# A state-space mixer on one core: the rows of B in their own PSUM bank, the block boundary in pieces

## The chip, the core and the metric

The kernel runs on one core of a Trainium2 chip. The core has five engines with instruction queues of their own: PE (matmul, with its weight loads shown apart as PEld), DVE (vector), ACT (activation functions), POOL (general vector work) and SP (here it only starts DMAs). Each engine works through its queue in order; semaphores make it wait for others. Matmul results land in PSUM, which has eight banks of 128 x 512 fp32; DVE and ACT read PSUM, POOL does not in this program. The metric is the time of one execution on the device in microseconds (us); of several runs the median is given.

## The reference, cut to what matters

The program is a stack of four layers, each a mixer and a feed-forward part, all with a residual and a norm before and after. The change touches the last mixer (a selective state-space model, "mamba") and the start of the feed-forward part behind it (routing to 8 experts). There are 8 batches of 512 tokens, width 256, inner width 512, 16 states. For each batch:

```python
xr = x @ W_in.T                       # x is the layernorm of the residual
xc, res = xr[..., :512], xr[..., 512:]
u = silu(depthwise_conv4(xc) + b_conv)
dt, B, C = split(u @ W_xproj.T)       # 16 + 16 + 16
delta = softplus(dt @ W_dt.T + b_dt)
dA = exp(delta * A)                   # per channel and state
dBu = delta * B * u
h_t = dA_t * h_(t-1) + dBu_t          # scan over 512 tokens
y = sum_n h * C + u * D
out = (y * silu(res)) @ W_out.T
x = x + layernorm(out)
```

The next part begins with `scores = softmax(layernorm(x) @ w_router)` and the two best experts of each token.

## The kernel before

Everything here is fp32. A block is one batch, b = 0 to 7; channels lie on the partitions in four chunks c of 128, tokens along the free dimension. `l3_attn` (L1545) walks a list of 128 pairs (b, n), a block's 16 states one after another (L1690).

**One state.** For each chunk ACT makes dA = exp(A dl) into PSUM (L1703, two tiles) and DVE scans it with dB into half of an h tile (L1706). POOL multiplies the two h tiles, 128 x 1024 each, by the row of C (L1709), and PE adds them into four PSUM banks y with an identity as weights (`summed`, L1677); this sum stands one state later in the program. h has six tiles, that is three states. What a scan takes is prepared two states ahead by `inputs` (L1642): the row of C comes by DMA from a DRAM copy of the projection, spread over the partitions (L1646, four tiles). For an even state PE spreads the row of B into PSUM with a one-column selection (pb, L1649) and DVE multiplies it by du (dB, L1652); for an odd state a DMA brings the row (L1656) and POOL multiplies (L1657).

**The next block's front.** `front` (L1590) is a generator that is stepped once per state while block b is scanned, and makes what block b+1 needs. It normalises x (`norm_act`: statistics on DVE, the scaling xn on ACT, L160), transposes it (L146, copied to xT, L148), and for each chunk projects (pi, L1585), copies to xc (L1596), convolves by four diagonal matmuls (pc, L1599) and copies to u with the bias (L1602). Then come Silu on u (L1604) with a load of ACT's table before and after it, the projection px (L1609), its copy xd and the DMA of xd to DRAM (L1616). For each chunk of delta one matmul pd (L1622), five ACT operations (L1627 to L1631) and three of DVE (L1633 to L1635) make the softplus dl. At last POOL forms du = dl u in one instruction of 128 x 2048 (L1638).

**The boundary.** In state 0 of block b the old block is finished: DVE gates y with sr (L1667), PE starts the new y with u D (L1715), `out` projects the old block back (py, L190) and `add_norm` (L164) takes statistics on DVE (L105 to L115, L170), scales on ACT (yn, L177) and adds to the residual X on POOL (L179). yn has the same buffer as xn. Then the gate of block b is projected (L1721, pi again) and goes through its own Silu (L1722), with two table loads.

**Banks.** PSUM is full: two banks "mm", two for dA, four for y. In "mm" stand pxT, pi, pc, px, pd, py and pb, in turn.

**Order.** The source order is a priority, not the queue: a scheduler at build time puts an instruction ahead where by its own reckoning its operands and buffers are there. So in the trace statistics of X for later blocks, and for the routing of the next part (`route`, L1812; `norm`, L126), stand amid the scans as soon as X is ready. Table loads keep their place in the program (L123).

Of the kernel before, what the change touches and what calls it, by code (L numbers as in the profile page):

```python
# [9 lines left out]
F32 = mybir.dt.float32  # L10
# [35 lines left out]
class Kern:  # L46


    def __init__(self, ctx, tc, i):
        self.ctx, self.tc, self.nc, self.i = ctx, tc, tc.nc, i  # L50
        nc = self.nc
        self.const = ctx.enter_context(tc.tile_pool(name="const", bufs=1))
        self.xpool = ctx.enter_context(tc.tile_pool(name="xres", bufs=1))
        self.wpool = ctx.enter_context(tc.tile_pool(name="wts", bufs=1))
        self.small = ctx.enter_context(tc.tile_pool(name="small", bufs=3))
        self.dram = ctx.enter_context(tc.tile_pool(name="dram", bufs=1, space=DRAM))
        self.C = self.const.tile([P, 384], F32, name="C")
        nc.sync.dma_start(out=self.C, in_=i["consts"][:, 0:384])
        self.ident = self.C[:, C_ID:C_ID + 128]
        self.caus = self.C[:, C_CAUS:C_CAUS + 128]  # L60
        self.up = self.C[:, C_UP:C_UP + 128]
        self.ones = self.const.tile([1, 128], F32, name="ones")
        nc.vector.memset(self.ones, 1.0)
        self.XA = self.xpool.tile([P, NB, NT, D], F32, name="X")
        self.X = [self.XA[:, b] for b in range(NB)]
        self.W = {}

        self.log_exp = False
        self.eps = self.const.tile([P, 1], F32, name="eps")
        nc.vector.memset(self.eps, LN_EPS)  # L70

# [51 lines left out]
        self.tc.keep_in_program_order(  # L123
            self.nc.scalar.preload_act_table_set("natural_log_exp_and_others"))

    def norm(self, b, pool):  # L126

        nc = self.nc
        x = self.X[b]
        mv, r = self.stats([x[:, n, :] for n in range(NT)], "ln")  # L130
        xn = pool.tile([P, NT, D], F32, tag="xn", name=f"xn{b}")
        for n in range(NT):
            nc.vector.tensor_scalar(
                xn[:, n, :], x[:, n, :], mv[:, n, 0:1], r[:, n:n + 1], ALU.subtract, ALU.mult)
        return xn
# [12 lines left out]
            nc.scalar.copy(xT[:, k, :], ps)  # L148
        return xT

    def norm_act(self, b, pool):

        nc = self.nc
        x = self.X[b]
        mv, r = self.stats([x[:, n, :] for n in range(NT)], "ln")
        nb = self.small.tile([P, NT], F32, tag="lnb", name="lnb")
        nc.vector.scalar_tensor_tensor(nb, mv[:, :, 0], -1.0, r, ALU.mult, ALU.mult)
        xn = pool.tile([P, NT, D], F32, tag="xn", name=f"xn{b}")
        for n in range(NT):
            nc.scalar.activation(  # L160
                xn[:, n, :], x[:, n, :], AF.Identity, bias=nb[:, n:n + 1], scale=r[:, n:n + 1])
        return xn
# [1382 lines left out]
def l3_attn(K):  # L1545

    nc, tc = K.nc, K.tc
    w = K.W["l3_attn"]  # L1550
    win = w[:, 0:2048].rearrange("p (k n) -> p k n", k=2)
# [3 lines left out]
    with ExitStack() as es:  # L1555
# [1 line left out]
            return es.enter_context(tc.tile_pool(name="l3" + name, bufs=bufs, **kw))  # L1557
        cst, s1, s2, s3 = pool("c", 1), pool("a", 1), pool("b", 2), pool("d", 3)
        s4, s6 = pool("h", 4), pool("g", 6)
        pmm = pool("pm", 2, space=PSUM)  # L1560
        pA = pool("pa", 2, space=PSUM)
        pY = pool("py", 1, space=PSUM)
        dr = pool("dr", 2, space=DRAM)
# [23 lines left out]
                    start=(k == 0), stop=(k == 1))  # L1587
            return ps

        def front(b, res):  # L1590
            xT = K.norm_T(
                b, s1, pmm, "mm", xn=K.norm_act(b, s1), dst=s1.tile([P, 2, L], F32, tag="xT", name=f"xT{b}"))
            yield
            u = s1.tile([P, 4, L], F32, tag="u", name=f"u{b}")
            for c in range(4):
                nc.scalar.copy(xc[:, 3:], project_in(b, c, xT))  # L1596
                pc = pmm.tile([P, L], F32, tag="mm", name=f"pc{b}_{c}")
                for s in range(4):
                    nc.tensor.matmul(  # L1599
                        pc, lhsT=dg[:, c, s, :], rhs=xc[:, 3 - s:3 - s + L],  # L1600
                        start=(s == 0), stop=(s == 3))
                nc.scalar.activation(u[:, c, :], pc, AF.Identity, bias=W[:, c, M_BC:M_BC + 1])  # L1602
                yield
            nc.scalar.activation(flat(u), flat(u), AF.Silu)  # L1604
            K.log_exp_tables()
            yield
            px = pmm.tile([48, L], F32, tag="mm", name=f"px{b}")
            for c in range(4):
                nc.tensor.matmul(  # L1609
# [7 lines left out]
            yield  # L1617

            dl = s2.tile([P, 4, L], F32, tag="dl", name=f"dl{b}")
            for c in range(4):  # L1620
                ps = pmm.tile([P, L], F32, tag="mm", name=f"pd{b}_{c}")
                nc.tensor.matmul(  # L1622
                    ps, lhsT=wdt[:, c * P:(c + 1) * P], rhs=xd[0:16, :], start=True, stop=True)
                bd = W[:, c, M_BD:M_BD + 1]
                e = s2.tile([P, L], F32, tag="e", name=f"e{b}_{c}")
                lg = s2.tile([P, L], F32, tag="lg", name=f"lg{b}_{c}")
                nc.scalar.activation(e, ps, AF.Abs, bias=bd)  # L1627
                nc.scalar.activation(dl[:, c, :], ps, AF.Relu, bias=bd)
                nc.scalar.activation(e, e, AF.Exp, scale=-1.0)
                nc.scalar.activation(ps, e, AF.Identity, bias=1.0)  # L1630
                nc.scalar.activation(lg, ps, AF.Ln)  # L1631

                nc.vector.scalar_tensor_tensor(ps, ps, -1.0, e, ALU.add, ALU.subtract)  # L1633
                nc.vector.tensor_tensor(ps, lg, ps, ALU.subtract)
                nc.vector.tensor_tensor(dl[:, c, :], ps, dl[:, c, :], ALU.add)  # L1635
                yield
            du = s2.tile([P, 4, L], F32, tag="du", name=f"du{b}")
            nc.gpsimd.tensor_tensor(flat(du), flat(dl), flat(u), ALU.mult)  # L1638
            res.update(xT=xT, u=u, dl=dl, du=du, xd=xd,
                       rows=xd_d.rearrange("(j n) t -> n j t", j=2))  # L1640

        def inputs(b, n):  # L1642
            du, xd, rows = res[b]["du"], res[b]["xd"], res[b]["rows"]
            dB = s3.tile([P, 4, L], F32, tag="dB", name=f"dB{b}_{n}")
            C = s4.tile([P, L], F32, tag="C", name=f"C{b}_{n}")
            nc.sync.dma_start(out=C, in_=rows[n, 1].partition_broadcast(P))  # L1646
            if n % 2 == 0:
                pb = pmm.tile([P, L], F32, tag="mm", name=f"pb{b}_{n}")
                nc.tensor.matmul(  # L1649
                    pb, lhsT=K.ident[0:48, 16 + n:17 + n].to_broadcast([48, P]), rhs=xd,  # L1650
                    start=True, stop=True)
                nc.vector.tensor_tensor(  # L1652
                    dB, du, pb[:, None, :].to_broadcast([P, 4, L]), ALU.mult)
            else:
                B = s2.tile([P, L], F32, tag="B", name=f"B{b}_{n}")
                nc.sync.dma_start(out=B, in_=rows[n, 0].partition_broadcast(P))  # L1656
                nc.gpsimd.tensor_tensor(  # L1657
                    dB, du, B[:, None, :].to_broadcast([P, 4, L]), ALU.mult)
            return dB, C

        def out(b, yT):
            K.project_out(
                b, [(yT[:, c, :], W[:, c, M_OUT:M_OUT + D]) for c in range(4)], pmm, "mm", s1, tag="xn")

        def gate(b, py, sr):
            for c in range(4):
# [3 lines left out]
        def summed(state):  # L1670
# [4 lines left out]
            for j, h in enumerate(hs):  # L1675
                for c in range(2):
                    nc.tensor.matmul(  # L1677
                        py[2 * j + c], lhsT=K.ident, rhs=h[:, c, :], start=False,
                        stop=(n == NS - 1))

        res = [{} for _ in range(NB)]
        for _ in front(0, res[0]):
            pass
        order = [(b, n) for b in range(NB) for n in range(NS)]
        ready = {k: inputs(*k) for k in order[:2]}
        py = sr = last = None
        nxt = iter(())
        for k, (b, n) in enumerate(order):  # L1690
            if n == 0:
                nxt = front(b + 1, res[b + 1]) if b + 1 < NB else iter(())
                dl, u = res[b]["dl"], res[b]["u"]
            if n == NS - 2:
                for _ in nxt:
                    pass
            dB, C = ready.pop((b, n))
            if k + 2 < len(order):
                ready[order[k + 2]] = inputs(*order[k + 2])
            hs = []  # L1700
            for c in range(4):
                dA = pA.tile([P, L], F32, tag="dA", name=f"dA{b}_{n}_{c}")
                nc.scalar.activation(dA, dl[:, c, :], AF.Exp, scale=A[:, c, n:n + 1])  # L1703
                if c % 2 == 0:
                    hs.append(s6.tile([P, 2, L], F32, tag="h", name=f"h{b}_{n}_{c}"))
                nc.vector.tensor_tensor_scan(  # L1706
                    hs[-1][:, c % 2, :], dA, dB[:, c, :], 0.0, ALU.mult, ALU.add)
            for h in hs:
                nc.gpsimd.tensor_tensor(h, h, C[:, None, :].to_broadcast([P, 2, L]), ALU.mult)  # L1709
            summed(last)  # L1710
            if n == 0:
                yT = gate(b - 1, py, sr) if b else None
                py = [pY.tile([P, L], F32, tag=f"y{c}", name=f"y{b}_{c}") for c in range(4)]
                for c in range(4):
                    nc.tensor.matmul(  # L1715
                        py[c], lhsT=dg[:, c, 4, :], rhs=u[:, c, :], start=True, stop=False)
                if b:
                    out(b - 1, yT)
                sr = s1.tile([P, 4, L], F32, tag="sr", name=f"sr{b}")
                for c in range(4):  # L1720
                    nc.scalar.copy(sr[:, c, :], project_in(b, 4 + c, res[b]["xT"]))  # L1721
                nc.scalar.activation(flat(sr), flat(sr), AF.Silu)  # L1722
                K.log_exp_tables()
            last = (py, hs, n)
            next(nxt, None)
        summed(last)
        out(NB - 1, gate(NB - 1, py, sr))
        K.log_exp = False


# [1 line left out]
def l3_ffn(K):  # L1732
# [18 lines left out]
    with ExitStack() as es:  # L1751
# [59 lines left out]

        def route(b, sb):  # L1812

            xn = K.norm(b, sb)
            nc.sync.dma_start(
                out=xn_d[b * L:(b + 1) * L].rearrange("(n p) d -> p n d", p=P), in_=xn)
            t = K.norm_T(b, sb, pmm, "mm", xn=xn, dst=TS[b])
# [340 lines left out]
```

## Time and profile before

| | us |
|---|---|
| median of 3 runs | 5200.95 |
| lowest and highest run | 5196.74, 5203.29 |
| the profiled execution | 5193.12 |
| its span, first to last instruction | 5191.4 |
| mean granted PE clock over the span | 0.927 of full |
| PE, DVE, ACT, POOL busy over the span | 4407.5, 3047.7, 1928.3, 1865.3 |
| scans (L1706), first to last start | 3431.7 to 4523.0 |
| C-products on POOL (L1709), last start | 4531.1 |

The times in a profile are of the one profiled execution; they are compared with its own span, not with the median. A group's line gives the code line, engine, operation, the tile written and those read, the shape and the count, then the busy time and the mean of one in ns, then the idle time of the engine just before them and what ended most of it. A wait is put down to what ended it, so an engine that waits in its queue also holds everything behind it. Busy spans of one engine can overlap by up to 0.1 us where instructions are pipelined. In the mixer the four y banks, the h tiles and the "mm" banks tie the engines together: each is handed on only when its last reader is done.

### The profile page before, as it was taken

How to read it: one execution, taken by the hardware profiler on the slowest of the kernel's cores; microseconds unless marked ns; L12 is line 12 of the kernel's file. 1: busy time of each engine (PE TensorE's matmuls, PEld its weight loads, DVE VectorE, ACT ScalarE, POOL GpSimd, SP SyncE). 2: the span in 40 equal slices, each digit the busy share in tenths (PEclk: the TensorE clock that was granted, in tenths of full speed). 3: DMA queues.
4: the chain of work that ended last, by engine and by line, in shares of the span. 5: the costliest groups of instructions: out<-in, count | busy, mean ns of one | idle time of the engine just before them, and what ended most of it. 6: DMA issues, size and time to landing. Idle time of an engine off the chain costs nothing.

```text
span 5191.4 us, 56559 instructions
## 1 busy us (share of the span) xinstructions
PE 4407.5 (85%) x18804; PEld 2700.6 (52%) x18804; DVE 3047.7 (59%) x8229; ACT 1928.3 (37%) x3817; POOL 1865.3 (36%) x1201
## 2 busy tenths in 40 slices
PE   8745789999983996988888899988888888899998
PEld 3334675565552894544444455533333333368885
DVE  7999646466687113555555653357778877761115
ACT  5401323434341332433333333355555555321112
POOL 0001213444342343111111110057889887803331
PEclk9876899999996997999999999999999999899999
DMA  4397411000001893000000000011111111126763
GB/s 113 80 208 176 132 47 48 5 5 9 5 17 42 225 253 97 5 5 5 5 5 5 1 20 1 0 43 42 45 45 49 45 43 43 47 80 216 227 214 101
DMA packets 401528, 357.89 MB, mean 69 GB/s; under 512 B 209394, under 2 KB 334020, under 8 KB 400676
## 3 DMA queue, kind: packets, MB, share of 16 engines
q1 hardware_dynamic: 373236, 305.83, 21.2%
q0 software_dynamic: 16320, 31.65, 2.2%
q10 hardware_dynamic: 11680, 16.80, 1.0%
q8 instruction: 149, 2.44, 0.2%
q14 instruction: 143, 1.17, 0.1%
HBM read 287.87 MB, written 66.09 MB: 68 GB/s over the span
## 4 chain that ended last, share of the span: by engine, by line
PE 34%; DVE 18%; issue 6%; POOL 5%; ACT 3%; DMA 1%; DVEq 0%; POOLq 0%; ACTq 0%; SPq 0%
DVE h L1706 7%; PE gb L1785 4%; PE T L1421 4%; PE h L1240 3%; DVE junk L1391 3%; PE g L1534 3%; PE y L1677 3%; PE yb L1799 2%; DVE dB L1652 2%; PE py L190 2%; PE pc L1599 2%; PE y L1251 2%; POOL h L1709 2%; PE o L1411 1%; PE pi L1585 1%
## 5 line engine op out<-in xcount | busy, mean ns | idle before, releaser
L1709 POOL TENSOR_TENSOR h<-h,C 128x1024 f32<-128x1024 f32 x256 | 596.2, 2357 | 178.2 <-DVE h L1706 140.0
L1677 PE MATMUL y<-h,C 128*128 128x512 f32 x1024 | 530.9, 659 | 104.6 <-POOL h L1709 104.6
L1706 DVE TENSOR_TENSOR_SCAN h<-dA,dB 128x512 f32<-128x512 f32 x512 | 589.4, 1204 | 29.4 <-ACT dA L1703 11.7
L1703 ACT ACTIVATE dA<-dl,A 128x512 f32<-128x512 f32 x512 | 352.5, 691 | 411.4 <-DVE h L1706 410.8
L935 POOL TENSOR_SCALAR p<-p,rs 128x128 f32<-128x128 f32 (+3 forms) x256 | 276.3, 1088 | 385.6 <-DVE rs L934 226.0
L1677 PEld LDWEIGHTS y<-h,C 128*128 128x128 f32 x1024 | 201.0, 207 | 410.9 <-issue 222.0
L1424 ACT ACTIVATE PT<-T 128x256 f32<-128x256 f32 (+3 forms) x512 | 208.5, 438 | 416.4 <-PE T L1421 409.8
L179 POOL TENSOR_TENSOR X<-X,yn 128x1024 f32<-128x1024 f32 x64 | 151.2, 2363 | 559.8 <-ACT yn L177 483.2
L1386 PE MATMUL S<-KT,qz 128*128 128x512 f32 (+3 forms) x1024 | 321.2, 453 | 22.4 <-DVE mx L1391 8.7
L1421 PE MATMUL T<-qz,KT 128*128 128x512 f32 (+3 forms) x1024 | 320.4, 445 | 12.0 <-ACT PT L1424 9.3
L1426 POOL TENSOR_SCALAR_AFFINE_SELECT PT<-PT 128x512 f32<-128x512 f32 x128 | 81.1, 637 | 609.8 <-ACT PT L1424 609.8
L1657 POOL TENSOR_TENSOR dB<-du,B 128x2048 f32<-128x2048 f32 x64 | 289.8, 4529 | 0.1
L1391 DVE CUSTOM_DVE_ANT_0 junk<-S,mask 128x256 f32<-128x256 f32 (+3 forms) x512 | 251.4, 491 | 61.9 <-PE S L1386 4.9
L1785 PE MATMUL gb<-xbT,w_b 128*128 128x256 f32 (+1 forms) x1472 | 255.3, 332 | 1.0 <-ACT ts L1989 0.6
L1386 PEld LDWEIGHTS S<-KT,qz 128*128 128x128 f32 x1024 | 180.4, 191 | 142.4 <-DVE mx L1391 30.7
L1652 DVE TENSOR_TENSOR dB<-du,pb 128x2048 f32<-128x2048 f32 x64 | 145.5, 2275 | 170.2 <-PE pb L1649 120.3
L1785 PEld LDWEIGHTS gb<-xbT,w_b 128*128 128x128 f32 x1472 | 230.2, 191 | 23.1 <-ACT ts L1989 0.8
L1791 DVE TENSOR_TENSOR hTb<-sb,gb 128x512 f32<-128x512 f32 x71 | 48.9, 688 | 325.3 <-PE gb L1785 325.3
L1421 PEld LDWEIGHTS T<-qz,KT 128*128 128x128 f32 x1024 | 169.1, 191 | 132.4 <-issue 66.5
L933 ACT ACTIVATE p<-p,nm 128x128 f32<-128x128 f32 (+3 forms) x256 | 143.8, 563 | 198.8 <-DVE nm L929 193.5
L1245 ACT ACTIVATE hT<-h,w_l_ffn 128x128 f32<-128x128 f32 x384 | 109.8, 368 | 220.3 <-PE h L1240 220.3
L1240 PE MATMUL h<-xgT,w 128*128 128x128 f32 x1536 | 185.0, 279 | 0.0
(506 smaller groups left out, 9132.7 us busy)
## 6 DMA issues: line engine op xcount, KB each, us to landing
w_b<-l3f_w SPq DMA_DIRECT2D x138, 512.0 KB
w<-l1f_w SPq DMA_DIRECT2D x48, 1024.0 KB
C<-xdd SPq DMA_DIRECT2D x128, 256.0 KB
B<-xdd SPq DMA_DIRECT2D x64, 256.0 KB
w<-l1f_w SPq DMA_DIRECT2D x48, 256.0 KB
toep<-l0fd SPq DMA_DIRECT2D x32, 320.0 KB
X<-x SPq DMA_DIRECT2D x16, 512.0 KB
toep<-l0fd SPq DMA_DIRECT2D x32, 256.0 KB
```

The source lines that it names most:

```text
L935: nc.gpsimd.tensor_scalar(p[:, 0:n], p[:, 0:n], rs, None, ALU.mult)
L1240: nc.tensor.matmul(ph[:, j, :], lhsT=w1[:, s, c, m * P:(m + 1) * P], rhs=xgT[:, c, :], start=(c == 0), stop=(c == 1))
L1386: nc.tensor.matmul(ps[:, 0:n], lhsT=QZ[:, j, qt * P:n], rhs=KT[:, g, 0:n], start=True, stop=True)
L1391: nc.vector.tensor_tensor_reduce(out=junk[:, 0:n], in0=tiles[j][:, 0:n], in1=mask[:, L - n:L], scale=1.0, scalar=-3.0e38, op0=ALU.add, op1 ...
L1421: nc.tensor.matmul(ps[:, 0:n], lhsT=KT[:, g, kt * P:(kt + 1) * P], rhs=QZ[:, j, kt * P:L], start=True, stop=True)
L1652: nc.vector.tensor_tensor(dB, du, pb[:, None, :].to_broadcast([P, 4, L]), ALU.mult)
L1657: nc.gpsimd.tensor_tensor(dB, du, B[:, None, :].to_broadcast([P, 4, L]), ALU.mult)
L1677: nc.tensor.matmul(py[2 * j + c], lhsT=K.ident, rhs=h[:, c, :], start=False, stop=(n == NS - 1))
L1703: nc.scalar.activation(dA, dl[:, c, :], AF.Exp, scale=A[:, c, n:n + 1])
L1706: nc.vector.tensor_tensor_scan(hs[-1][:, c % 2, :], dA, dB[:, c, :], 0.0, ALU.mult, ALU.add)
L1709: nc.gpsimd.tensor_tensor(h, h, C[:, None, :].to_broadcast([P, 2, L]), ALU.mult)
L1785: nc.tensor.matmul(ps[:, q, :], lhsT=ww[:, k, (c + q) * P:(c + q + 1) * P], rhs=xT[:, k, :], start=(k == 0), stop=(k == 1))
```

## The change

- PSUM: "mm" has one bank, and a pool "pb" of one bank holds the rows of B of even states.
- `inputs` is split. `rows_of` (DMA of C, and B by PE or DMA) runs three states ahead, `product` (dB) two ahead; both now stand after a state's four scans, where `inputs` stood before them.
- `front` is stepped after the second scan of each state but the first, not at a state's end. xn is written into the upper half of the tile that u will fill. A chunk's conv and the next chunk's projection form one piece. The gate's Silu of block b and the Silu of u of block b+1 stand together. lg lies in du's chunk, e has one tile, and du is formed chunk by chunk (four of 128 x 512). The gate's projection for b+1 is the last piece.
- `among` wraps this: norm of b+1, then the projection back of b-1 (now with leave=True, so ACT first copies the two PSUM halves to SBUF, L175), then the rest of `front`.
- In the last block, where there is no front, `among` makes the statistics of X[0] to X[6] for the next part, one batch per state, each behind a fence: a DVE memset that keeps its place in the program. They are copied to constant tiles, and `route` takes them from there.

The core of the diff:

```diff
+    def fence(self):
+        t = self.small.tile([P, 1], F32, tag="fence", name="fence")
+        return self.tc.keep_in_program_order(self.nc.vector.memset(t, 0.0)).ins
+
-        mv, r = self.stats([x[:, n, :] for n in range(NT)], "ln")
+        mv, r = known or self.stats([x[:, n, :] for n in range(NT)], "ln")
...
-        pmm = pool("pm", 2, space=PSUM)
+        pmm = pool("pm", 1, space=PSUM)
+        pB = pool("pb", 1, space=PSUM)
...
+            u = s1.tile([P, 4, L], F32, tag="u", name=f"u{b}")
+            xn = K.norm_act(b, s1, u[:, 2:4, :].rearrange("p c t -> p (c t)").rearrange(
+                "p (n d) -> p n d", n=NT))
+            yield
...
-            nc.scalar.activation(flat(u), flat(u), AF.Silu)
+            for t in (sr, u):
+                if t is not None:
+                    nc.scalar.activation(flat(t), flat(t), AF.Silu)
             K.log_exp_tables()
...
-            nc.gpsimd.tensor_tensor(flat(du), flat(dl), flat(u), ALU.mult)
+                nc.gpsimd.tensor_tensor(du[:, c, :], dl[:, c, :], u[:, c, :], ALU.mult)
+            yield
+            for c in range(4):
+                nc.scalar.copy(res["sr"][:, c, :], project_in(b, 4 + c, xT))
+                if c == 1:
+                    yield
...
+        def among(b, yT):
+            sr = res[b]["sr"]
+            ahead = front(b + 1, res[b + 1], sr) if b + 1 < NB else iter(())
+            next(ahead, None)
+            if b:
+                out(b - 1, yT)
+            yield
+            if b + 1 < NB:
+                yield from ahead
+            else:
+                nc.scalar.activation(flat(sr), flat(sr), AF.Silu)
+                K.log_exp_tables()
+                for d in range(NB - 1):
+                    yield
+                    mv = K.const.tile([P, NT, 2], F32, name=f"fmv{d}")
+                    r = K.const.tile([P, NT], F32, name=f"fr{d}")
+                    K.known.append((mv, r))
+                    with tc.issue_after(K.fence()):
+                        m, t = K.stats([K.X[d][:, n, :] for n in range(NT)], "ln")
+                        nc.vector.tensor_copy(mv, m)
+                        nc.vector.tensor_copy(r, t)
...
+                if n and c == 1:
+                    next(nxt, None)
...
+            if k + 2 < len(order):
+                ahead = order[k + 2]
+                dBs[ahead] = product(*ahead, rows[ahead][0])
+            if k + 3 < len(order):
+                rows[order[k + 3]] = rows_of(*order[k + 3])
```

## The prediction

> **What bounds it now.** I read the share table first, and it misleads: over the span PE is busiest, but the change lies in the state-space mixer alone, from about 3368 to 4545 us of the profiled execution (the stretch where the scan's line appears). So I took that stretch by blocks. The scans' starts in order of time give block starts at 3431.7, 3550.0, 3693.2, 3836.4, 3979.6, 4123.5, 4266.8 and 4410.3: block 0 takes 118.2 us, the six blocks after it 143.2 to 143.9 (mean 143.4). The view by stretches has block 0, block 2 and block 7 to the end of POOL's work (length, then busy us and count of PE, PEld, DVE, ACT, POOL, then the granted clock):
>
> ```profile
> 3431.70:3550.00 118.30, 104.76 (x223) 39.57 (x221) 95.49 (x85) 70.41 (x104) 107.56 (x40) 0.95 0.19 51
> 3693.20:3836.40 143.20, 124.19 (x273) 50.53 (x272) 107.86 (x116) 75.93 (x115) 116.82 (x43) 0.92 0.18 45
> 4410.30:4533.40 123.10, 97.36 (x204) 41.20 (x202) 97.16 (x90) 52.56 (x76) 114.99 (x43) 0.86 0.14 42
> ```
>
> POOL carries the most: 116.8 of 143.2 us. It is 32 products with C, 8 odd dB, du and one residual add, in the page's rows:
>
> ```profile
> L1709 POOL TENSOR_TENSOR h<-h,C 128x1024 f32<-128x1024 f32 x256 | 596.2, 2357 | 178.2 <-DVE h L1706 140.0
> ...
> L1657 POOL TENSOR_TENSOR dB<-du,B 128x2048 f32<-128x2048 f32 x64 | 289.8, 4529 | 0.1
> ...
> L1652 DVE TENSOR_TENSOR dB<-du,pb 128x2048 f32<-128x2048 f32 x64 | 145.5, 2275 | 170.2 <-PE pb L1649 120.3
> ```
>
> The last row shows the cause: DVE lost 120 us to pb. Who waited in block 2, POOL's three waits and DVE's largest two (total, times, longest):
>
> ```profile
> POOL h L1709 <- DVE h L1706: 22.5, 4, 18.1
> POOL h L1709 <- DVE onb L170: 2.8, 1, 2.8
> POOL h L1709 <- PE pb L1649: 1.1, 1, 1.1
> ```
>
> ```profile
> DVE dB L1652 <- PE pb L1649: 15.9, 2, 12.0
> DVE dB L1652 <- POOL du L1638: 6.4, 1, 6.4
> ```
>
> So POOL idles 26.4 us per middle block, 18.1 at once. The chain of waits through that hole (start, us, what):
>
> ```profile
> 3726.31 2.31 POOL X L179
> 3728.62 0.03 issue
> 3728.65 0.60 ACT xn L160
> ...
> 3729.77 3.71 PE pi L1585 x8
> ...
> 3741.74 3.52 PE pc L1599 x8
> 3745.26 1.06 PE pb L1649 x2
> 3746.32 0.02 issue
> 3746.34 2.30 DVE dB L1652
> ```
>
> A row of B (pb) takes its bank from the ring "mm" that pxT, pi, pc and py use. Here it queues behind the next block's front; the front waits for xn, whose buffer is still yn until the add to X; and DVE holds scans behind the dB that wants pb. Block 0 has the same front but no block before it to finish, and no such hole: its first eight states take 58.5 us, block 2's 84.3; its last eight 59.7, block 2's 58.9.
>
> **The change, part by part.** *B rows in an own bank, three ahead; norm in u; no hoisted routing statistics.* These cut every link of that chain: pb needs only the even dB of two states before; xn no longer waits for the add; and the next layer's statistics (bn_stats on X, where DVE idles 4.9 us for the add in block 2) are fenced into block 7. POOL's floor becomes 32 x 2.31 (starts of products back to back) + 8 x 4.49 + 2.30 + du. du in pieces: 2.357 at 1024 and 4.529 at 2048 give 0.18 + 2.12 per 1024, so 1.24 for 512, 5.0 for four instead of 4.5. Floor 117.1. For what idles above it I take block 0's halves: 58.5 + 2.3 (add) + 2.8 (DVE's onb wait stays) + 59.0 + 0.5 = 123.1. With 1 us for the ring below: **124 per middle block, 19.4 less, six times: -116**. Ends: floor and 2 us (119), and 143.
>
> *Ring of one bank instead of two.* Per block it is handed on 21 times (2 pxT, 8 pi, 4 pc, px, 4 pd, 2 py). A handover is an ACT copy and two hops, 0.9 to 1.0 us by the first front's rows (pc ends, u copied in 0.69, pi starts); a pd is five ACT operations (3.2) and three DVE (2.1), 5.3. PE itself needs 108 us at full clock: 233 passes of 512 columns 0.43 apart, 32 of 256 at 0.216, 8 transposes. Wholly bare: 17 x 1.0 + 4 x 5.3 = 38, so 146 per block; wholly hidden: 0. The cover is the y matmuls (64 x 0.86 us) and three states of h buffers; steps are one per state of about 7 us, so I take 1. Where it is bare PE stands in order, y and then h buffers behind it.
>
> [...] The row first: block 0 was granted 0.95, but the first front, where the ring runs alone (3368 to 3431.7), 0.79. At 0.79, 108 us become 137 and the gain falls to 6.4 a block; at 0.95, 114, and POOL stays the bound. I take 0.95, since y fills the gaps as in block 0.
>
> *Gate's projection last, one Silu.* Two table loads a block go (2 x 1.28 on ACT, which is half idle), but u's and the gate's Silu stand together: 1.28 + 2 x 1.91 + 1.28 = 6.4 us in which ACT makes no dA; two dA tiles cover 2.2, and h done ahead most of the rest. Nothing by the row (DVE waits 1.4 at the present Silu), at most 4. The 8 matmuls move from state 0 to 13 and 14, where PE has room (4 x 0.86 of 7 us).
>
> *leave=True:* two ACT copies, 0.58 each; hidden. *Queues:* SP issues C for state k+3 once h of k-1 is done; its product is one h pair (4.7 us) later than now and so is its use, so nothing changes; the write of xdd at state 7 can queue behind one C and is wanted at 13. On POOL a du piece waits for dl with the products behind it: 0, since POOL runs behind DVE there; at worst 2.1 each. xn in u waits for block b's D matmuls, with dA behind it on ACT: they end as state 1 begins; at most 2.
>
> *First front,* bare by nature: four pd one after another at 6.6 (1.0 + 3.2 + 2.1 + hops) instead of 16.1 for all, +10; ring for pxT and pc, +3.5; last du piece 1.2 instead of 4.5, -3.2; the gate's copies gone from block 0's first state, -1: **+9** (0 to 15). Block 0: +1.
>
> *Seven statistics in block 7.* Own DVE work each: 4 x 0.33 + 4 x 0.07 + 3 small + 2 copies + memset, 2.2. The three small operations read two SBUF operands. The row for them beside a busy POOL:
>
> ```profile
> L113 DVE SCALAR_TENSOR_TENSOR onh<-onmv,ony x7: 1968/2132/4371, 3573.5 to 4431.7; 128x4 f32<-128x4 f32 x7
> ```
>
> It takes 0.16 where POOL is idle, yet 2.43 in the mean here, each time to the end of POOL's running instruction. [...] Sum 7 x (2.2 + 2.6) = 34 by the row, 64 by the rule. DVE has 25.9 idle in block 7, so +8 or +38; minus 1 for pb's remaining holes there, **+7**. This is what stands against the gain.
>
> *Next layer without seven statistics:* some 4 us of DVE each, but PE is busy 39.8 of 40 us from 4560 on with the shared expert. -2 (0 to -28). Last output with one bank: +1.
>
> **Sum:** -116 + 9 + 1 + 7 - 2 + 1 = -100, from 5191.4 (span) to 5091. The run around it was 5193.12, the median 5200.95; so 5101 against the median.
>
> **Rivals.** (A) Better: 119.5 a block, the fence harmless, first front +6: -143 + 6 + 1 - 2 + 1 = -137, **5064**. For it: last eight states already run at 59; against: onb's wait. (B) The ring shows partly: three handovers in ten bare, 11 us, about 134: -56 + 16 = -40, **5161**. For it: PE is in order and its first eight states carry about 63 us of work against POOL's 56; against: block 0 carries as much in 58.5. (C) Slower: the ring bare, nearly all of the 38 us, with pd's 5.3 the heaviest: 148 per block, +28 + 16 = +44, **5245**. It decides from 1.6 us per handover in the mean, (143.4 - 16/6 - 108)/21. For it: PE's order is fixed, so a bare handover stops the y matmuls too; against: with two banks block 0's PE waited at most 3.4 us in all for xc, 2.1 for dl, 1.5 for u. (D) It does nothing because another wait (du's 6.4, py) ends last: 5195 to 5205.
>
> **Chances.** Forecast (5075 to 5130) 0.50, A 0.18, B 0.18, C 0.11, D 0.03. Runs of this kernel lie within 6.6 us, so 0.2% (10 us) is what can be told: faster 0.86, within 0.03, slower 0.11. Range 5050 to 5170 leaves out C, D and the tails of A and B.
>
> **What would show it.** Block starts 122 to 126 apart from block 1 on; no wait of dB on pb over 2 us; POOL's idle per middle block 5 to 9 us, mostly behind L113; POOL's counts unchanged but du x32 at 1.24; granted clock 0.93 or more there; first scan at about 3441; L113 and L115 of the fenced statistics at 2 us and more, and block 7 at 120 (to its last scan). Wrong it is if PE waits for ACT u, ACT xc or DVE dl over 10 us per block with the clock under 0.85 (B, C), or if block 7 takes over 140.

## The result, and the profile after

The kernel after takes **5240.61 us** in the median of 4 runs (5237.26 to 5246.9), against 5202.12 for the one before in the same comparison: ratio 1.0077, 95% interval 1.006 to 1.0095. It is slower by 0.8%, where I forecast 5101. The profiled execution has a span of 5235.9 us, 44.5 more than before. The starts of the scans say where:

| stretch, us | before | after | difference | forecast |
|---|---|---|---|---|
| start to the first scan | 3431.7 | 3446.4 | +14.7 | +9 |
| block 0 | 118.2 | 126.5 | +8.3 | +1 |
| blocks 1 to 6 | 860.4 (143.4 each) | 864.0 (144.0 each) | +3.6 | -116 |
| block 7, first to last scan | 112.7 | 129.6 | +16.9 | +7 |
| after the last scan | 668.4 | 669.4 | +1.0 | -1 |

So the six middle blocks, which were to pay for everything, gave nothing. The view by stretches of the kernel after, blocks 0, 2 and 7 (length, busy us and count of PE, PEld, DVE, ACT, POOL, then clock, DMA share and GB/s):

```profile
3446.40:3572.90 126.50, 112.14 (x239) 43.01 (x240) 103.84 (x97) 71.62 (x108) 112.78 (x45) 0.95 0.19 51
3718.80:3866.00 147.20, 126.21 (x274) 52.59 (x274) 113.07 (x102) 79.00 (x119) 117.42 (x46) 0.91 0.16 44
4437.00:4566.50 129.50, 86.08 (x164) 33.13 (x164) 127.97 (x180) 55.56 (x90) 99.71 (x37) 0.82 0.12 37
```

Block 2's busy times hardly moved: POOL 117.4 us as against 116.8, at a clock of 0.91 against 0.92. Little work was added (DVE 113.1 against 107.9 us, ACT 79.0 against 75.9); idle time mostly changed its place. Block 7 is another case: DVE is busy for 128.0 of 129.5 us. The page's row of the scan before, then those of scan and product after (the lines L1706 and L1709 of before):

```profile
L1706 DVE TENSOR_TENSOR_SCAN h<-dA,dB 128x512 f32<-128x512 f32 x512 | 589.4, 1204 | 29.4 <-ACT dA L1703 11.7
```

```profile
L1752 DVE TENSOR_TENSOR_SCAN h<-dA,dB 128x512 f32<-128x512 f32 x512 | 595.8, 1206 | 189.2 <-PE y L1704 103.2
L1765 POOL TENSOR_TENSOR h<-h,C 128x1024 f32<-128x1024 f32 x256 | 597.2, 2352 | 181.1 <-DVE h L1752 142.6
```

The product's row is as before, idle time and all (178.2 before). The scan's is not: DVE's idle time ahead of it went from 29.4 to 189.2 us, 103.2 of it for the sums y on PE. DVE's idle time as a whole is about what it was, in block 2 147.2 - 113.1 = 34.1 us against 35.3; before, most of it stood ahead of dB. Block 2's waits, POOL's largest two and DVE's largest three (total, times, longest):

```profile
POOL h L1765 <- DVE h L1752: 23.2, 8, 5.2
POOL du L1659 <- DVE dl L1658: 2.7, 1, 2.7
```

```profile
DVE h L1752 <- PE y L1704: 15.5, 5, 5.8
DVE h L1752 <- ACT dA L1749: 11.6, 5, 6.5
DVE dB L1683 <- PE pb L1673: 2.5, 2, 2.2
```

The wait for pb is down from 15.9 to 2.5 us: that part does what it says. In its place DVE waits for y (the h tiles are full) and for dA. By states, from one state's first scan to the next, block 2 took:

| state | 0 | 1 | 2 | 3 | 4 | 5 | 6 | 7 to 14 | 15 |
|---|---|---|---|---|---|---|---|---|---|
| before | 12.3 | 4.5 | 9.1 | 29.7 | 4.5 | 10.8 | 4.5 | 63.5 | 4.5 |
| after | 6.7 | 11.8 | 7.8 | 5.2 | 11.0 | 15.5 | 15.4 | 53.9 | 20.0 |

The hole of 29.7 us is gone. Its time is not: states 0 to 6 together take 73.4 us, where they took 75.2, since states 4 to 6 have grown by 22. States 7 to 14 take 9.6 us less, and state 15 takes 15 more. The chain of waits through state 15 (start, us, what):

```profile
3843.15 2.35 POOL h L1765
...
3845.54 6.96 PE y L1704 x10
3852.51 1.06 PE pd L1644 x2
...
3853.59 0.69 ACT e L1649
...
3857.39 2.37 POOL h L1765
...
3859.80 1.14 PE y L1704 x2
...
3860.96 0.69 DVE sr L1694
3861.65 0.61 DVE dl L1658
...
3862.40 1.27 POOL du L1659
...
3863.70 2.30 DVE dB L1683
```

Here the last of the four softplus chunks, pd on PE, starts only at the block's end, behind y sums; DVE reaches its dl behind the old block's gate (sr), and du, dB and the new block's scans wait for dl. POOL and the scans run dry. In block 4 the four pd start 85.1, 97.7, 112.2 and 127.9 us into the block. The dl that gives the single bank back ends at 97.6, 109.6 and 122.2 us: no pd starts before that, and the last two start another 2.6 and 5.7 us after it, as they stand behind y sums in PE's queue. Before, with two banks, the last dl was done at 124.1 us; now at 137.7, with a block of 141.4.

### The profile page after: what moved, and what is told of

The parts are those of the page before. It is cut to its first block, busy times and chain, and to the rows that moved or that the text cites. A ratio compares the mean times of both kernels' runs of the same rounds, so it can differ in the third digit from the quotient of the medians.

```text
span 5235.9 us, 56676 instructions
## 1 busy us (share of the span) xinstructions
PE 4429.6 (85%) x18804; PEld 2705.3 (52%) x18804; DVE 3096.9 (59%) x8180; ACT 1953.2 (37%) x3859; POOL 1868.7 (36%) x1225
## 4 chain that ended last, share of the span: by engine, by line
PE 34%; DVE 17%; issue 7%; ACT 4%; POOL 4%; DMA 1%; DVEq 0%; POOLq 0%; ACTq 0%; SPq 0%
DVE h L1752 5%; PE gb L1834 4%; PE T L1428 4%; PE h L1247 3%; DVE junk L1398 3%; PE y L1704 3%; PE g L1541 3%; PE yb L1848 2%; PE py L197 2%; PE pc L1615 2%; PE y L1258 2%; POOL h L1765 1%; PE o L1418 1%; PE pi L1594 1%; PE gs L1834 1%
## 5 line engine op out<-in xcount | busy, mean ns | idle before, releaser
L1752 DVE TENSOR_TENSOR_SCAN h<-dA,dB 128x512 f32<-128x512 f32 x512 | 595.8, 1206 | 189.2 <-PE y L1704 103.2
L1765 POOL TENSOR_TENSOR h<-h,C 128x1024 f32<-128x1024 f32 x256 | 597.2, 2352 | 181.1 <-DVE h L1752 142.6
L1252 ACT ACTIVATE hT<-h,w_l_ffn 128x128 f32<-128x128 f32 x384 | 109.8, 368 | 218.9 <-PE h L1247 218.9
L1247 PEld LDWEIGHTS h<-xgT,w 128*128 128x128 f32 x1536 | 176.7, 193 | 0.0
```

What stands on the lines that cost most here:

```text
L1247: nc.tensor.matmul(ph[:, j, :], lhsT=w1[:, s, c, m * P:(m + 1) * P], rhs=xgT[:, c, :], start=(c == 0), stop=(c == 1))
L1752: nc.vector.tensor_tensor_scan(hs[-1][:, c % 2, :], dA, dB[:, c, :], 0.0, ALU.mult, ALU.add)
```

## The experiments

Theory: the single bank. A softplus chunk holds it from pd over five ACT operations that stand among the dA, and three DVE operations that stand among scans, and the four chunks in series come too late. Rivals: the pieces' place in the program (after the second scan, so ahead of a state's y sums), and the statistics in block 7. "Middle block" is the mean of blocks 1 to 6; every ratio is against the kernel before.

### The bank alone, on the kernel before

```diff
-        pmm = pool("pm", 2, space=PSUM)
+        pmm = pool("pm", 1, space=PSUM)
+        pB = pool("pb", 1, space=PSUM)
...
-                pb = pmm.tile([P, L], F32, tag="mm", name=f"pb{b}_{n}")
+                pb = pB.tile([P, L], F32, tag="pb", name=f"pb{b}_{n}")
```

(and leave=True in `out`).

> The kernel before with one part of the change: pb has its own bank, "mm" one bank (and leave=True, which one bank needs). Ring theory (the chain of handovers of the single "mm" bank sets the block): the hole at pb goes, but middle blocks stay at 138 to 152 us, the first front grows by 10 us or more, in all 5200 to 5290. Rival 1 (placement: the pieces amid the scans and their order on PE cost the time, not the bank): middle blocks fall to about 125, in all 5090 to 5120. Rival 2 (waits of DVE's two-operand SBUF instructions for POOL): as rival 1.

5225.87 us, ratio 1.0051 (1.0034 to 1.0067); a middle block takes 145.9, as the ring theory expected. The hole shrank from 29.7 to 16.7 us and state 15 grew from 4.5 to 18.2. In block 2 DVE waits for y as in the kernel after:

```profile
DVE h L1707 <- PE y L1678: 16.1, 4, 4.9
```

DVE's wait for y and the long state 15 thus come with the bank alone; the long states 4 to 6 do not (19.5 us here, 19.8 before).

### The change with two banks

```diff
-        pmm = pool("pm", 1, space=PSUM)
-        pB = pool("pb", 1, space=PSUM)
+        pmm = pool("pm", 2, space=PSUM)
...
-                B = pB.tile([P, L], F32, tag="pb", name=f"pb{b}_{n}")
+                B = pmm.tile([P, L], F32, tag="mm", name=f"pb{b}_{n}")
```

> The changed kernel with one part undone: "mm" has two banks again and the rows of B share them. Ring theory: middle blocks fall from 144 to 130 or less, block 0 from 126.5 to about 119, the first scan comes 8 us or more earlier, in all 5090 to 5160. Rival 1 (placement) and rival 2 (DVE waits for POOL): middle blocks within 3 us of 144, in all 5220 to 5250.

5173.0 us, ratio 0.9949 (0.9933 to 0.9966). A middle block takes 135.3, state 15 again 4.5 us. I had expected 130 or less, and 5160 at most: the bank is a smaller part of the loss than the theory said, though far more than either rival allows. DVE's wait for y in block 2:

```profile
DVE h L1751 <- PE y L1703: 5.9, 2, 3.8
```

All else of the change is thus worth 143.4 - 135.3 = 8.1 us per middle block, and the bank costs 144.0 - 135.3 = 8.7.

### Without the seven statistics in block 7

```diff
-                for d in range(NB - 1):
+                for d in range(0):
```

> The changed kernel without the seven fenced statistics in block 7; the next layer makes them itself. All theories: block 7 (first to last scan) falls from 129.6 to 112 to 116. Ring theory: middle blocks stay within 3 us, in all 5220 to 5226. If the fence was what kept the middle blocks from being worse, they rise by 3 us or more each.

5230.38 us, ratio 1.0061 (1.0044 to 1.0078). Block 7 took 102.1 us in place of 129.6, less than the 112 to 116 expected, and the time lies above the 5220 to 5226 expected, since the scheduler then put the work amid other scans: the bn_stats of one batch into each of blocks 1 to 6, and 27 small operations behind them into block 4, which took 157.3 us in place of 141.4. After the last scan it took 669.4 us, as with the fenced statistics: the next layer gains nothing from them. Block 7 by stretches without them:

```profile
4451.70:4553.80 102.10, 77.89 (x165) 31.97 (x165) 95.81 (x83) 51.98 (x76) 99.43 (x37) 0.89 0.14 47
```

DVE has 102.1 - 95.8 = 6.3 us free there. The statistics' rows in the kernel after, block 7 (lowest, median, longest ns):

```profile
L116 DVE SCALAR_TENSOR_TENSOR lnw<-lnh,lny x7: 131/1418/1426, 4466.9 to 4535.3; 128x4 f32<-128x4 f32 x7
L1730 DVE COPY fr<-lnw x7: 156/157/3410, 4469.5 to 4538.8; 128x4 f32<-128x4 f32 x7
L1729 DVE COPY fmv<-lnmv x7: 141/157/2299, 4463.5 to 4532.9; 128x8 f32<-128x8 f32 x7
```

Of the 35 small operations and copies of the seven statistics, 12 take 1.3 to 3.4 us, each beside a running POOL instruction; the others take 0.13 to 0.16. Their seven rows in that stretch sum to 40.5 us, and DVE has nowhere to put them.

### Four more handovers of the bank

```diff
+                ex = pmm.tile([P, L], F32, tag="mm", name=f"ex{b}_{c}")
+                nc.tensor.matmul(
+                    ex[:, 0:8], lhsT=wdt[:, c * P:(c + 1) * P], rhs=xd[0:16, 0:8], start=True, stop=True)
+                nc.scalar.copy(exs, ex[:, 0:8])
```

(after each softplus chunk; exs is read by nobody.)

> The changed kernel with four more handovers of the "mm" bank in each front: after each softplus chunk one matmul of 8 columns into the bank and a copy of 8 columns by ACT, next to no work. Ring theory: each costs 1 to 4 us, so middle blocks +4 to +16 us, in all +30 to +110. Rivals 1 and 2: under 1.5 us per block, in all under +10.

5236.35 us in a single run, a middle block of 142.7. Four more short stays in the bank cost a middle block nothing that shows; in the first front, with no scans beside it, and in block 0 the times are 3.2 and 3.8 us longer. My theory in its first form, a price for every handover, fell here; what was left was how long a tile stays.

### Two banks, and the statistics behind the last scan

The loop over d goes from `among` to behind the last state; else as with two banks.

> As b_two_banks, with the seven fenced statistics moved from block 7 to behind the last scan, where POOL is idle. Theory (they cost block 7 because DVE, in order, waits for POOL's running instruction and for ACT): block 7 falls from 136 to 105 to 115, what follows the last scan grows by 0 to 10 us, in all 5140 to 5155. Rival (block 7 is long for another reason): over 125, in all 5165 or more.

5155.24 us, ratio 0.9914 (0.9897 to 0.993). Block 7 fell from 136.0 to 109.8; after the last scan it took 673.0 in place of 666.8.

### Two banks, statistics last, the front behind the y sums

```diff
-                if n and c == 1:
-                    next(nxt, None)
...
             last = (py, hs, n)
+            if n:
+                next(nxt, None)
```

(the rest of the generator is run out at state 14.)

> As e_end_stats, with the front stepped at the end of a state (behind the y sums) as before, not after its second scan. If the place of the pieces amid the scans costs time (they stand ahead of y on PE, h buffers run out): middle blocks fall by 4 us or more below e_end_stats. If the place helps: they rise by 4 us or more. Within 3 us: it does not matter.

5122.6 us, ratio 0.9845 (0.9829 to 0.9862): a middle block of 130.7. The pieces' place ahead of y cost 4.6 us per block. Two of DVE's waits in block 2:

```profile
DVE h L1741 <- PE y L1703: 9.1, 3, 3.8
DVE dB L1682 <- PE pb L1672: 6.1, 3, 3.3
```

### A softplus chunk in one piece

```diff
                 nc.scalar.activation(lg, ps, AF.Ln)
-                yield
...
                 nc.gpsimd.tensor_tensor(du[:, c, :], dl[:, c, :], u[:, c, :], ALU.mult)
-            yield
+                yield
```

(on the kernel after.)

> The changed kernel, one bank, with a softplus chunk in one step (ACT and DVE part together) instead of split over two states. Chunk theory (the bank is held some 13 us by each of four softplus chunks, so the last one ends behind the old block's gate and the pipeline drains in state 15): state 15 falls from 20 us to under 14 and middle blocks by 4 to 14. Rival (state 15 is long for another reason): within 2 us of 144.

5244.35 us in a single run, a middle block of 144.0, and in block 4 the four pd within 0.1 us of the kernel after. What I expected did not come: state 15 stays at 20.0 us, and the rival's figure is the one measured. The split over two states is not what makes a chunk late. That the bank is, this run does not show.

### One softplus chunk less

```diff
+                if c == 3:
+                    nc.scalar.copy(dl[:, 3, :], dl[:, 2, :])
+                    yield
+                    nc.gpsimd.tensor_tensor(du[:, c, :], dl[:, c, :], u[:, c, :], ALU.mult)
+                    continue
```

> The changed kernel, leaving out the fourth softplus chunk: dl of chunk 3 is a copy of chunk 2 by ACT. Work left out per block: PE 0.9, ACT 2.6, DVE 2.0 us. Chunk theory: the bank is free 13 us earlier, state 15 falls from 20 us to 5 to 9, middle blocks by 9 to 15, in all 60 to 105 us less than the changed kernel. Rival (engine work bounds): at most 2 to 3 us per block, in all under 20.

5175.4 us in a single run, a middle block of 133.8, 10.2 less, and state 15 down from 20 to 11.2 (5 to 9 expected). The kernel leaves a part of the function out, so this is a test of the cause and no version to keep. What was left out is short: 0.9 us on PE, 2.6 on ACT, 2.0 on DVE. A chunk costs a block about twice the sum of its work.

### The square: one bank, the front behind the y sums

The version of 5122.6 us with the first edit's two pools.

> The version with two banks, statistics behind the last scan and the front stepped behind the y sums (5122.6, 130.7 us per middle block), but again with one bank mm and an own bank for the rows of B. It closes the square: one bank and pieces ahead of y 144.0, two and ahead 135.3, two and behind 130.7. Theory (each of the four softplus chunks holds the single bank for about 13 us, and four of them in series are late for the block's end): state 15 again takes 12 to 20 us, against 10.4, and a middle block 138 to 143; time 5170 to 5205. Rival (the harm came from pieces that stood ahead of y on PE, and the bank alone costs nothing): a middle block within 1 us of 130.7 and the time within 10 us of 5123.

5190.6 us, ratio 0.9976 (0.9966 to 0.9985). A middle block:

| us | pieces ahead of y | pieces behind y |
|---|---|---|
| one bank | 144.0 | 139.3 |
| two banks | 135.3 | 130.7 |

The bank costs 8.7 and 8.6, the place 4.7 and 4.6: two separate losses that add up. Blocks 5 and 6 alone say nearly the same: 7.6 and 7.0, 5.0 and 4.5. The rival, that the bank alone is harmless, falls. DVE waits for y 13.8 us in block 2 here. Its wait for dA goes with the place: 2.1 us here, where the kernel after had 11.6. Where in a block the two losses lie (means of blocks 1 to 6, us):

| states | 0 to 6 | 7 to 14 | 15 |
|---|---|---|---|
| kernel before | 75.3 | 63.7 | 4.5 |
| one bank, ahead (kernel after) | 70.2 | 54.2 | 19.6 |
| two banks, ahead | 70.7 | 60.1 | 4.5 |
| one bank, behind | 65.8 | 55.5 | 18.0 |
| two banks, behind | 63.0 | 57.4 | 10.4 |

With the pieces ahead, the bank's cost is all in state 15, which grows by 15.1 us while states 7 to 14 shrink by 5.9; with the pieces behind, state 15 grows by 7.6. That is where a late softplus chunk shows. The place costs 4.4 us with one bank and 7.7 with two in states 0 to 6, where the closed hole should have shown as a gain.

### The gate's projection of the first front behind the first products

```diff
-        for _ in front(0, res[0]):
-            pass
+        ahead = front(0, res[0])
+        for _ in range(12):
+            next(ahead)
...
         dBs[order[1]] = product(*order[1], rows[order[1]][0])
+        for _ in ahead:
+            pass
```

(on the version of 5122.6 us.)

> The version with two banks, statistics behind the last scan and the front stepped behind the y sums, and in the first front alone the gate's projection placed behind the first rows and products. Theory (its twelve matmuls stand ahead of the first row of B on PE and cost about 7 us of the way to the first scan, of which some 2 us come back as late gate work): first scan 4 to 7 us earlier after the add to X, time 5116 to 5119. Rival (the last softplus chunk sets the first scan anyway): under 1 us, 5122.

**5116.08 us, ratio 0.9833 (0.9817 to 0.9849)**, the lowest time of all, though its interval overlaps that of the version before it. From the add to X to the first scan it took 69.0 us in place of 76.9: with two banks the projection (eight matmuls, not twelve) stood ahead of the first pb, which starts at 3442.7 us there and at 3426.2 here. Block 0 gave 4.6 of it back; block 1 took 129.5 in place of 137.2, which I did not follow up.

### The norm in the place of u, alone, on the kernel before

```diff
+            u = s1.tile([P, 4, L], F32, tag="u", name=f"u{b}")
+            xn = K.norm_act(b, s1, u[:, 2:4, :].rearrange("p c t -> p (c t)").rearrange(
+                "p (n d) -> p n d", n=NT))
             xT = K.norm_T(
-                b, s1, pmm, "mm", xn=K.norm_act(b, s1), dst=s1.tile([P, 2, L], F32, tag="xT", name=f"xT{b}"))
+                b, s1, pmm, "mm", xn=xn, dst=s1.tile([P, 2, L], F32, tag="xT", name=f"xT{b}"))
```

> The kernel before with one edit: the normalised x is written into the upper half of the tile that u will fill, so that it no longer waits for yn to be added to X. Theory (the hole of 29.7 us is the row of B that queues behind the whole front in the ring, and the wait of xn for the add is only its start, 3 to 5 us): the hole stays at 22 us or more and a middle block falls from 143.4 to 138 to 142, time 5165 to 5195. Rival (the add to X is the link that makes the front late; with it cut the front runs beside state 2): the hole falls under 12 us, a middle block to 125 to 131, time 5075 to 5125.

5222.02 us, ratio 1.0038 (1.0024 to 1.0052); blocks 5 and 6 take 143.2 and 143.6 as before, blocks 1 to 4 are 4 to 6 us longer, so the saving that the theory allowed did not come either. The hole is 31.4 us. From its chain of waits in block 2, which starts at 3705.6:

```profile
3739.40 9.51 PE pi L1586 x16
...
3753.25 1.28 ACT L124
3754.53 0.01 issue
3754.54 0.59 ACT xT L148
...
3755.18 1.12 PE pi L1586 x2
...
3757.16 3.52 PE pc L1602 x8
3760.68 1.07 PE pb L1652 x2
```

The norm is early now (16 us into the block, 35 before), and pb starts no earlier than before: it still queues in the ring, behind the gate's projection, its Silu with table loads, xT, pi and pc. The link that held the hole in block 2 was the ring, not the add to X.

### The bank given back early

```diff
+                ps = res["sr"][:, c, :]
                 nc.scalar.activation(ps, e, AF.Identity, bias=1.0)
```

(on the kernel after: 1 + e and the three DVE operations go to a free chunk of sr, so pd's bank is free after two ACT operations.)

> The kernel after with one line more: 1+e and the three DVE operations of a softplus chunk use the free chunk of sr in SBUF, so the pd matmul gives its bank back after two ACT operations and not after the last DVE operation. Bank count, number of handovers, order and amount of work stay. Theory (the harm is the 13 us for which each softplus chunk holds the one bank): the four pd come within about 30 us, state 15 falls from 20 to 12 or less and a middle block from 144.0 to 132 to 138, although twelve DVE operations now take two SBUF operands beside POOL and may each wait up to 2.3 us; time 5165 to 5205. Rival (handovers as such, or ACT's and DVE's places for the softplus, set the drain): state 15 stays at 18 to 20 us, a middle block at 143 to 147, time 5235 to 5255.

5236.1 us, ratio 1.0072 (1.0056 to 1.0089); a middle block of 142.4. Half of the theory's expectation came: state 15 fell from 20 to 4.5 us, and from the first pd to the last dl it takes 37.1 us in block 4, against 52.6 after and 33.5 before. The time did not follow and lies where the rival had it; in block 2 state 10 rose from 9.2 to 16.8 and state 12 from 6.3 to 10.7. The first DVE operation of the chunk in block 2, in the kernel after and in this one:

```profile
L1656 DVE SCALAR_TENSOR_TENSOR pd<-pd,e x4: 672/675/691, 3816.1 to 3858.7; 128x512 f32<-128x512 f32 x4
```

```profile
L1657 DVE SCALAR_TENSOR_TENSOR sr<-sr,e x4: 659/1492/4979, 3805.9 to 3831.6; 128x512 f32<-128x512 f32 x4
```

With both operands in SBUF it took 4.98 us once, 4.3 more than in the kernel after; that this is a wait for POOL, as with the statistics in block 7, is my estimate. The twelve operations of block 2 take 16.0 us where they took 8.1. Of the 7.6 us that state 10 grew, 6.9 are time added to these operations; of state 12's 4.4, 1.0, and what holds the rest I did not follow. So the stay in the bank makes the drain of state 15, as the theory has it. That a shorter stay would also shorten the block, this run does not show, as its own cost nearly ate the gain. The same with the scratch in PSUM was not to be had, as all eight banks are taken.

## Why the prediction was wrong

- **The step that failed is "Ring of one bank instead of two", taken at 1 us per block.** It cost 8.7 (the square). A middle block took 20.0 us more than the 124 forecast: 7.7 are this step, 4.6 the pieces' place, and 7.6 a saving that was summed too large, whose cause stays open (below). My ends, 0 and 38, held it, and the choice near zero was wrong in its reason: I took the y sums and three states of h as cover. They are the victims. PE takes its queue in order, so y stands behind a pi or pc that waits for the bank, the six h tiles fill, and DVE waits for y: 15.5 us in block 2 of the kernel after and 13.3 to 16.1 in that of five other versions with one bank, against 5.9 and 9.1 in the two of the square with two.
- **A pd was priced at 5.3 us bare, 6.6 with hops**, the sum of eight operations run back to back. Amid the scans it stays 9.8 to 12.5 us in the bank, and the next starts 12.6 to 15.7 after it, since the operations stand in the queues of ACT and DVE among dA and scans, and the next pd in PE's among y sums. Four in series take 52.6 us in place of 33.5, and the block ends without its du. That the length of the stay and not the number of handovers matters rests on three runs: four short stays more cost a middle block nothing, one chunk less gave 10.2 us, and an early release took state 15 back to 4.5.
- **The 19.4 us saved per block.** The cutting of pb's link held (2.5 us of waits left). The add to X, the other link of the chain that I read, was not what made the hole: with that link alone cut, it was 31.4 us long. "Block 0's halves" did not hold: even with two banks and the pieces behind y a middle block takes 130.7, and in the best version 129.6, where I summed 123.1. With two banks and the pieces ahead of y it is 135.3; 4.6 of that is a place that I did not price at all. The front's step now stands after the second scan, ahead of the state's y sums; I asked whether PE has room for it, and not what waits behind it. The last 6 us all lie in the first eight states: in block 2 of the best version these take 70.2 us, where I had summed 63.6, and the last eight 59.4 against 59.5. What holds them was not tried; in block 1 of that version DVE waits 9.1 us for y, 6.4 for pb and 3.1 for du.
- **Gate's projection last, one Silu: two table loads fewer forecast, two more came.** Each of blocks 1 to 6 has six, where the kernel before has four. The two Silu stand together in the source and not in the trace: the scheduler put the gate's (sr) 62 us ahead of u's. The call that loads the tables for exp and log stands behind u's alone. So behind the gate's Silu the next dA loads a table itself, then the statistics' L112 loads one, and dA behind it again. ACT's table loads in block 2 of the kernel after:

```profile
3735.70 1.28 ACT L1624 ACT_TABLE_LOAD   x1
3738.93 1.28 ACT L1749 ACT_TABLE_LOAD   x1
...
3752.14 1.28 ACT L112 ACT_TABLE_LOAD   x1
3753.75 1.28 ACT L1749 ACT_TABLE_LOAD   x1
...
3798.13 1.28 ACT L1624 ACT_TABLE_LOAD   x1
3801.35 1.28 ACT L125 ACT_TABLE_LOAD   x1
```

That is 4 x 1.28 = 5.1 us of ACT per block more than I counted. All four versions of the square have six, so the square stands. In the best version four of the six lie in block 2's first eight states, and DVE waits there 2.4 us for a statistics operation of ACT that stands behind one of them. They are a candidate for a part of the last 6 us; no run tried it.
- **Seven statistics: +7 forecast, +16.9 measured.** The sum of the work is near, 40.5 us in the rows against my 34, but in part by luck. The 2.6 us of waits per batch in my 34 are read from the boundary's norm in the kernel before: L113 waits always (2.3), L114 once in seven (2.27 us against 0.16), L115 never there. The 64 beside it takes three waits of 2.3 us in every batch, which no run shows. In block 7 the three small operations waited eight times of 21, 12.3 us in all, where I had 18, and not those that I had named: the third (L116 now), which was never to wait, waited in five of seven, and the first (L114 now), which was always to wait, in two. The two copies, whose waits I had at nothing, waited four times of 14, 10.8 us; I had counted only the three operations with two operands. What failed is the cover. I set the work against 25.9 us of idle DVE, read over the 123.1 us to the end of POOL's work. To the last scan, for which the +7 stands, DVE of the kernel before is idle for 112.7 - 95.1 = 17.6 us:

```profile
4410.30:4523.00 112.70, 87.21 (x186) 37.20 (x185) 95.06 (x87) 52.56 (x76) 104.59 (x39) 0.86 0.15 46
```

13.2 us of that were waits for pb, which the same change removes. Without the statistics that block takes 102.1 us, 10.6 less than before, with 6.3 of DVE idle; with them it takes 27.5 more.
- **First front:** +9 forecast. From the add to X to the first scan +11.7, another 2.9 arose before the mixer. The last dl comes 15.0 later, near what was priced (13.5). **Block 0:** +1 forecast, +8.3; it has the same four chunks, its state 15 takes 20.1 us in place of 4.5. **Next layer and last output:** -1 forecast, +1.0.
- **The clock:** 0.91 in block 2 and 0.95 in block 0, near the 0.95 that I chose and far from the 0.79 of the first front before. From 3431 to 4400 us the kernel before was granted 0.93, the one after 0.92, and the version of 5116.08 us, with two banks, 0.96.
- **Signs.** The named sign, PE waiting over 10 us for u, xc or dl at a clock under 0.85, did not come, though the bank was the cause: in block 2 PE waited 4.0 us for u and 0.5 for dl. The loss shows on DVE, as waits for y and dA.
- **Rival C** gave 5245 and is near by coincidence: it adds nearly all of 38 us per block for the bare ring to PE's own 108, where the bank cost 8.7, and has neither the pieces' place nor the open 7.6 us.

## What to carry to other kernels

Price a PSUM tile by its stay, from the matmul's start to the end of its last reader in the real queues, and not by the sum of its readers (here 9.8 to 12.5 us, not 5.3); then lay these stays in series if the ring has one bank. The other work in an engine's queue was no cover for a stall here: the y sums stood behind the waiting instruction on PE, and DVE waited 15.5 us for them in block 2. And where one edit removes an idle time, no other edit of the same change may be hidden in it. Last, what stands side by side in the source need not do so in the queue, as the two Silu show.

## What the runs showed of the hardware

In block 7 of the kernel after, 12 of the 35 small operations and copies of the statistics took 1.3 to 3.4 us in place of 0.13 to 0.16. Each of the 12 started while a POOL instruction ran and ended 0.02 to 0.03 us after one ended; 21 of the other 23 started with POOL idle, the last two 0.05 to 0.06 us before its instruction ended. Four of the 12 are copies of 128 x 4 and 128 x 8, with one operand: they waited as the eight with two operands did. One of them, and the POOL instruction that it waited for:

```profile
4504.78 4.50 POOL L1683 TENSOR_TENSOR dB<-du,B 128x2048 f32<-128x2048 f32 x1
...
4505.90 3.41 DVE L1730 COPY fr<-lnw 128x4 f32<-128x4 f32 x1
```

Where the softplus went to SBUF, POOL's instructions took longer too, in the mean over the run: a product of 128 x 1024 2416 ns in place of 2352, and du of 128 x 512 1580 in place of 1263.
